# Gated block of a transformer stack: norms of later sequences placed beside the blocks of a square layer, and two more steps run ahead of a branch

## The chip, the cores and the metric

The kernel runs on one core of one Trainium2 chip. The metric is the device time of one launch in microseconds (us), the median of several runs. A core has a matrix engine (PE; its weight loads are listed as PEld), a vector engine (DVE), a scalar engine (ACT), GpSimd (POOL) and SyncE (SP), which here issues the DMAs. Each engine takes its instructions in the order in which the program emits them, and they wait for each other through semaphores.

## What is computed

Eight sequences of 512 positions by 128 features pass six layers of attention with a small MLP, and then a gated block. The change touches the gated block and the seam before it. Cut to what matters (`attn` is the six layers, `norm` subtracts the mean and divides by the root of variance plus 1e-5; `s1`, `s2`, ... are scales of each output feature):

```python
def reference(x, ...):                      # x: 8 x 512 x 128, f32
    x = x + attn(norm(x))
    v = norm(x)
    h = silu((v @ W1.T) * s1) * ((v @ W2.T) * s2)   # 128 -> 512
    h = gelu((h @ H1.T) * t1)                       # 512 -> 512
    h = gelu((h @ H2.T) * t2)                       # 512 -> 512
    return x + (h @ W3.T) * s3                      # 512 -> 128
```

The matrices W1, W2, H1 and H2 hold only -1, 0 and 1 in this input. The kernel looks at their low 12 bits at run time and takes the first of two arms of a branch (`gated_split`) if all are zero; that arm is the one that runs here.

## The kernel before, in words

**Attention.** The six layers of eight sequences are 48 units of 32 steps each. A step makes two score tiles on PE, takes their row maxima on DVE and their exponentials on ACT. All other work of a unit (projections, mixing, norms, MLP) is cut into small functions that are filed in the dictionary `later` under a step number and a place (`at`, L646); when the loop comes to a step, it emits what is filed there (`pending`, L652). A unit's work reaches some 76 steps past its own scores, so when the scores of the last unit end at step 1535, work is still filed from step 1536 on: the last mixing of the last unit, and the norms and MLPs of the last three units. `plan_group` (L735) and `plan_after` (L716) file it. Step 1536 holds one `gather` (L473) of the last unit and the `aggregate` of a norm; step 1537 holds `weights` (L462) of the last group of scores and `mix_values` and `mix_end` (L498, L506) of the last but one block of rows.

**Seam.** `finish(upto)` (L818) emits everything filed up to a step, in order. It is called with 1535, then the register with the low bits is read and the branch follows. What is left in `later` is emitted inside the arm, one step at a time, by `next_step` (L825).

**Gated block.** One `Gate` (L514) per sequence b has four stages. Stage 0 (`gate_stage`, L567) has four blocks; a block is four matmuls (named `q`), a silu on ACT (`sils`), a product on DVE (`gt`, L578) and a split. The split (L543) cuts a tile into a high and a low part: DVE masks the high part (`cut`, L549), POOL copies it into place (L550), and DVE subtracts it (L551); the parts are named `vs`, `fgs`, `h1s` by their tile. Stage 1 (`hidden_stage`, L584, the first square layer) has four blocks of eight matmuls (`qh`, L562), a gelu on ACT (`ht`, L598) and a split into `h1s`. Stage 2 (second square layer) has four blocks of eight matmuls and a gelu into `g`, with no split. Stage 3 (`end`, L603) has 32 matmuls (`fo`, L608), a product on DVE (`y`, L615), an addition on POOL (L619) and the DMA to `out`. After each block `run_stage` calls `next_step`, so that leftover steps lie between blocks. PSUM tiles of the matmuls come from a ring of six (`ring`, L179); transposes, MLP products and some others share one more (`one`, L176).

**The norm of a sequence** (`Gate.norm`, L530) is five calls in a row: `add` (L522; POOL adds the attention result to a fresh copy of x, the tile `x_out`, and makes the tile `v`), `stats` (four DVE statistics, L194), `aggregate` (four on DVE, L200, then two small POOL instructions, L201 and L202), `centre` (POOL, L205) and `scale` (POOL, L210). `turn` (L537) then transposes `v` on PE (`pt_w`, L217) and ACT copies it to `vT` (L541); `split_input` (L553) splits it into `vs` for stage 0. Gates 0 and 1 have had their norm in the attention loop; gates 2 to 7 get theirs in `gated_split` (L877).

**Order in `gated_split`.** Iteration b emits stage 0 of b, the whole norm of b+1, stage 2 of b-1, the turn and the split of b+1, stage 1 of b, stage 3 of b-1, and the load of `x_out` for b+2. `done(b)` (L831) names a step by which the attention result of b is complete; `finish(done(b+1))` stands ahead of the norm.

Of the kernel before, what the change touches and what calls it, by code (L numbers as in the profile page):

```python
# [9 lines left out]
F32 = mybir.dt.float32  # L10
# [7 lines left out]
P = 128  # L18
# [11 lines left out]
def attn_stack_then_ffn(ctx: ExitStack, tc: tile.TileContext, a: dict, out: bass.AP):  # L30
# [3 lines left out]
    B, L, E = x.shape  # L34
# [4 lines left out]
    LC = L // P  # L39
# [11 lines left out]
    work = ctx.enter_context(tc.tile_pool(name="work", bufs=2))  # L51
# [43 lines left out]
    def load_x(b, n):  # L95
        t = state.tile([P, LC, E], F32, tag="x", name=f"x_{n}", bufs=3)
        nc.sync.dma_start(t, x[b].rearrange("(c p) e -> p c e", p=P))
        return t
# [77 lines left out]
    def one(shape, n):  # L176
        return ps_one.tile(shape, F32, tag="one", name=n)
# [49 lines left out]
    U = len(units)  # L227
    PAIRS = LC * STRIPS * 2
# [285 lines left out]
    class Gate:  # L514
# [7 lines left out]
        def add(self):  # L522
            b = self.b
            self.x = xs.pop(b)
            nc.gpsimd.tensor_tensor(self.x, self.x, hs[b][:, :, 0:E], ALU.add)
            tag, bufs = ("vf", 1) if b < 2 else ("z1", None)
            self.v = work.tile([P, LC, E], F32, tag=tag, name=f"v_{b}", bufs=bufs)
            self.ln = Norm(self.x, self.v, f"f{b}")

        def norm(self):  # L530
# [107 lines left out]
    gates = [Gate(b) for b in range(B)]  # L638
# [107 lines left out]
    def step_rest(s):  # L746
        pending(s, PE_)
        pending(s, DVE_)
        pending(s, ACT_)

    def step_ring(s):
        for fn in later.pop((s, RING_), ()):
            fn()()
# [10 lines left out]
    xs = {}  # L764

    def load_out(b):
        if b < 2:
            xs[b] = load_x(b, f"out{b}")
        elif b < B:
            tag = ("hik", "lok", "hiq")[b % 3]  # L770
            xs[b] = work.tile([P, LC, E], F32, tag=tag, name=f"x_out{b}", bufs=1)
            nc.sync.dma_start(xs[b], x[b].rearrange("(c p) e -> p c e", p=P))

    for k in range(2 + 2 * HC):
# [4 lines left out]
    for b in range(2):  # L779
        gate, t = gates[b], (U - 2 + b) * PAIRS  # L780
        at(t - 4, DVE_, lambda b=b: load_out(b))
        at(t + 9, DVE_, gate.add)
        at(t + 14, DVE_, lambda gate=gate: gate.ln.stats(0, 2))
        at(t + 15, DVE_, lambda gate=gate: gate.ln.stats(2, LC))
        at(t + 26, DVE_, lambda gate=gate: gate.ln.aggregate())
        at(t + 28, DVE_, lambda gate=gate: gate.ln.centre())
        at(t + 29, DVE_, lambda gate=gate: gate.ln.scale())
# [30 lines left out]
    def finish(upto):  # L818

        for s in sorted({s for s, _ in later}):  # L820
            if s <= upto:
                step_rest(s)
                step_ring(s)

    def next_step():  # L825
        if later:
            s = min(s for s, _ in later)
            step_rest(s)
            step_ring(s)

    def done(b):  # L831

        return (U - B + b + 4) * PAIRS + 12

    def gated(b):
# [14 lines left out]
        for wt, sc, nm in ((fh1, "f_h1s_col", "h1"), (fh2, "f_h2s_col", "h2")):  # L850
            pool, tag = (proj, "qs") if nm == "h1" else (epool, "e")
            g2 = pool.tile([P, HC, L], F32, tag=tag, name=f"{nm}_{b}")
            for o in range(HC):
                ph = ring([P, L], f"p{nm}_{b}_{o}")
                for c in range(HC):
                    nc.tensor.matmul(
                        ph, wt[:, c, o * P : (o + 1) * P], gg[:, c, :],
                        start=(c == 0), stop=(c == HC - 1),
                    )
                nc.scalar.activation(g2[:, o, :], ph, AF.Gelu, scale=cols[sc][:, o : o + 1])  # L860
                if o == HC - 1 and 1 < b + 1 < B:
                    if nm == "h1":
                        load_out(b + 1)
                        finish(done(b + 1))
                        gates[b + 1].norm()
                    else:
                        gates[b + 1].turn(one([P, L], f"pt_v{b + 1}"))()
                next_step()
            gg = g2
        gates[b].end(gg)  # L870

    def run_stage(b, k):
        if 0 <= b < B:
            for _ in gates[b].stage(k):
                next_step()

    def gated_split():  # L877

        load_out(2)
        gates[0].split_input()  # L880
        next_step()
        for b in range(B + 1):
            run_stage(b, 0)
            if 1 < b + 1 < B:
                finish(done(b + 1))
                gates[b + 1].norm()
            run_stage(b - 1, 2)
            if b + 1 < B:
                if b + 1 > 1:
                    gates[b + 1].turn(one([P, L], f"pt_w{b + 1}"))()  # L890
                gates[b + 1].split_input()
            run_stage(b, 1)
            run_stage(b - 1, 3)
            if b + 2 > 2:
                load_out(b + 2)

    finish(U * PAIRS - 1)
    wide = nc.values_load(
        low_any, min_val=0, max_val=1 << 12,
        skip_runtime_bounds_check_because="it only chooses between two arms",  # L900
# [4 lines left out]
    with tc.If(wide < 1) as narrow:  # L905
        gated_split()
# [65 lines left out]
```

## Time and profile before

| | |
|---|---|
| median of 3 runs | 2724.29 us (2723.52 to 2725.32) |
| the profiled execution: its time | 2724.5 us |
| the profiled execution: its span, first to last instruction | 2722.4 us |
| mean granted PE clock, share of full speed | 0.992 |
| PE, DVE, ACT, POOL busy, share of the span | 97%, 91%, 92%, 69% |
| first matmul of stage 0 of sequence 0 | 2470.63 us after the start of the span |
| starts of stage 0 of sequences 4, 5, 6, 7 | 2590.38, 2620.57, 2651.01, 2681.76 us |

The span is the time between the first and the last instruction of one profiled execution; 2.1 us of the launch lie outside it. A share of busy time is a mean over two very different parts: about 2470 us of attention, in which the change alters nothing, and about 252 us of leftover steps and gated block, to which it belongs. The second part has to be read by its own rows, with a window that holds it alone. In a row of waits the engine named first stood idle until the instruction named after the arrow was done; columns are the total in us, the number of times and the longest.

### The profile page before, as it was taken

Reading aid. Unit: us, or ns where it says so; the run is one execution under the profiler, and the core shown is the slowest. Engines: PE = TensorE matmul, PEld = TensorE weight load, DVE = VectorE, ACT = ScalarE, POOL = GpSimd, SP = SyncE. Lnnn points to the kernel's source line nnn. Section 1 sums busy time; section 2 is a strip of 40 time slices with the busy share of each in tenths; the row PEclk is TensorE's granted clock in tenths of the full one; section 3 lists DMA queues with packets and bytes.
Section 4 is the critical chain, followed back from the end, with each engine's and each line's share of the span. In section 5 each row is a group of like instructions: output and inputs, shape, how many; then the busy total and the mean of one; then the engine's idle time right before and its main releaser. Section 6 shows DMA issues by size and latency. Waiting matters only on the chain.

```text
span 2722.4 us, 52066 instructions
## 1 busy us (share of the span) xinstructions
PE 2635.7 (97%) x14944; PEld 1377.4 (51%) x14944; DVE 2490.1 (91%) x6109; ACT 2495.2 (92%) x6846; POOL 1882.6 (69%) x2278
## 2 busy tenths in 40 slices
PE   6999999999999999999999999999999999998988
PEld 2445445445545545445445445445445445445776
DVE  6999999999999999999999999999999999997653
ACT  6999999999999999999999999999999999996343
POOL 5677777676676676676676676776776676676754
PEclk9999999999999999999999999999999999999989
DMA  6545444445444445444445444445445545440000
GB/s 147 116 104 133 96 107 109 100 103 125 101 102 109 99 104 126 104 98 109 102 101 126 105 98 108 107 98 124 106 100 119 124 118 132 110 93 5 16 16 21
DMA packets 135859, 273.78 MB, mean 101 GB/s; under 512 B 39696, under 2 KB 57232, under 8 KB 135568
## 3 DMA queue, kind: packets, MB, share of 16 engines
q1 hardware_dynamic: 133504, 269.31, 42.6%
q8 instruction: 122, 2.00, 0.3%
q10 hardware_dynamic: 2064, 1.08, 0.2%
q14 instruction: 169, 1.38, 0.2%
HBM read 13.86 MB, written 2.10 MB: 6 GB/s over the span
## 4 chain that ended last, share of the span: by engine, by line
PE 44%; ACT 32%; DVE 16%; issue 5%; POOL 2%; DMA 0%; ACTq 0%; SPq 0%; POOLq 0%; DVEq 0%
ACT e L455 27%; PE ps L441 13%; PE acc L476 12%; DVE top L450 11%; PE py L404 6%; PE po L501 3%; PE qh L562 3%; ACT g L394 2%; ACT w L483 2%; PE pk L260 2%; PE fo L608 1%; PE pt_w L217 1%; PE pq L269 1%; PE pt_h L217 1%; PE pt_u L217 1%
## 5 line engine op out<-in xcount | busy, mean ns | idle before, releaser
L455 ACT ACTIVATE e<-ps,top 128x512 f32<-128x512 f32 x3072 | 2125.0, 823 | 31.4 <-DVE top L450 15.0
L450 DVE TENSOR_REDUCE top<-ps 128x1 f32<-128x512 f32 x3072 | 1947.9, 680 | 35.6 <-PE ps L441 29.2
L441 PE MATMUL ps<-ks,qs 128*128 128x512 f32 x3040 | 1225.9, 477 | 25.6 <-ACT e L455 17.8
L455 ACT ACTIVATION_READ_ACCUMULATOR e<-ps,top 128x1 f32 x3072 | 1050.2, 342 | 0.0
L441 PEld LDWEIGHTS ps<-ks,qs 128*128 128x128 f32 x3040 | 489.3, 189 | 869.3 <-ACT e L455 652.6
L476 PE MATMUL acc<-e,rp 128*32 128x512 f32 x6144 | 819.1, 605 | 0.8 <-POOL rp L466 0.3
L466 POOL TENSOR_TENSOR rp<-pick,r 128x128 f32<-128x128 f32 x768 | 308.9, 402 | 532.5 <-DVE r L464 206.0
L476 PEld LDWEIGHTS acc<-e,rp 128*32 128x32 f32 x6144 | 121.2, 108 | 261.1 <-issue 134.1
L315 POOL TENSOR_TENSOR m<-loq,mask 128x512 f32<-128x512 f32 x190 | 243.2, 1280 | 0.0
L315 POOL TENSOR_TENSOR m<-hiq,mask 128x512 f32<-128x512 f32 x190 | 242.8, 1278 | 0.0
L501 PEld LDWEIGHTS po<-h,wT 128*128 128x128 f32 x1536 | 201.2, 192 | 20.1 <-DVE wT L493 3.9
L501 PE MATMUL po<-h,wT 128*128 128x129 f32 x1536 | 204.1, 276 | 1.0 <-DVE wT L493 1.0
L392 PE MATMUL pf<-uT,w 128*128 128x512 f32 x384 | 196.3, 592 | 0.3
L404 PEld LDWEIGHTS py<-w,g 128*128 128x128 f32 x1536 | 186.0, 192 | 10.8 <-DVE z L411 1.9
L404 PE MATMUL py<-w,g 128*128 128x128 f32 x1536 | 187.2, 275 | 1.0 <-DVE z L411 1.0
L394 ACT ACTIVATE g<-pf,b_col 128x512 f32<-128x512 f32 x192 | 164.8, 859 | 3.3 <-PE pf L392 3.3
L483 ACT ACTIVATE w<-acc 128x512 f32<-128x512 f32 x192 | 131.8, 686 | 22.3 <-PE acc L476 22.3
L464 DVE RECIPROCAL r<-zs 128x4 f32<-128x4 f32 x768 | 129.2, 168 | 4.4 <-ACT e L455 0.7
L493 DVE TENSOR_TENSOR wT<-pt_w,decay 128x512 f32<-128x512 f32 x192 | 126.9, 661 | 0.2
L279 POOL TENSOR_TENSOR loq<-qT,hiq 128x512 f32<-128x512 f32 x48 | 61.6, 1283 | 87.8 <-ACT e L455 67.1
L217 PE MATMUL pt_w<-ident,w 128*128 128x128 f32 x768 | 120.2, 279 | 0.6
L217 PEld LDWEIGHTS pt_w<-ident,w 128*128 128x128 f32 x768 | 88.2, 140 | 43.5 <-ACT g L394 30.1
(115 smaller groups left out, 2522.9 us busy)
## 6 DMA issues: line engine op xcount, KB each, us to landing
qs<-m SPq DMA_DIRECT2D x1520, 128.0 KB, 2.4
ks<-hik SPq DMA_DIRECT2D x384, 64.0 KB, 2.0
ks<-lok SPq DMA_DIRECT2D x376, 64.0 KB, 2.0
rows<-in_rows SPq DMA_DIRECT2D x6, 448.0 KB, 4.9
x_in<-in_x SPq DMA_DIRECT2D x8, 256.0 KB, 3.2
fh<-square SPq DMA_DIRECT2D x8, 256.0 KB, 2.3
x_out<-in_x SPq DMA_DIRECT2D x8, 256.0 KB, 3.0
out<-y SPq DMA_DIRECT2D x7, 256.0 KB, 2.4
```

What stands on the lines that cost most here:

```text
L217: nc.tensor.transpose(pt[:, c * P : (c + 1) * P], src[:, c, :], ident)
L315: nc.gpsimd.tensor_tensor(m[:, lc - 2 * two], part.unsqueeze(2).to_broadcast([P, NB, PER_STRIP, QB]), mask.unsqueeze(1).to_broadcast([P, N ...
L392: nc.tensor.matmul(pf, w1[:, f * P : (f + 1) * P], self.uT, start=True, stop=True)
L394: return lambda: nc.scalar.activation(self.g[:, f, :], pf, AF.Relu, bias=cols["b1_col"][:, k : k + 1])
L404: nc.tensor.matmul(self.py[:, k, :], self.g[:, f, c * P : (c + 1) * P], w2[:, f, :], start=(f == 0), stop=(f == FC - 1),)
L441: nc.tensor.matmul(ps[s], qs[:, nb * P : (nb + 1) * P].bitcast(F32R), un.ks[:, i, :].bitcast(F32R), start=True, stop=True,)
L450: nc.vector.tensor_reduce(top[s], ps[s], AX.X, ALU.max, negate=True)
L455: nc.scalar.activation(self.e[:, nb, :], ps[s], AF.Exp, bias=top[s], accum_out=self.zs[:, nb : nb + 1],)
L466: nc.gpsimd.tensor_tensor(self.rp, pick.unsqueeze(1).to_broadcast([P, NB, QB]), r.unsqueeze(2).to_broadcast([P, NB, QB]), ALU.mult,)
L476: nc.tensor.matmul(acc[nb * QB : (nb + 1) * QB, :], self.rp[:, nb, :], self.e[:, nb, :], start=(self.turn == 0), stop=(self.turn == STRIPS ...
L483: nc.scalar.activation(self.w.rearrange("p c l -> p (c l)"), acc, AF.Exp, scale=1.0 / H)
L501: nc.tensor.matmul(self.po, self.wT[:, c, :], self.unit.h[:, c, 0 : E + 1], start=(c == 0), stop=(c == LC - 1),)
```

## The change

In four parts:

1. **The norm is spread.** The norm of b+1 between stage 0 of b and stage 2 of b-1 goes. In its place the norm of b+2 is handed to stage 1 of b as a list of four functions (`norm_beside`): `add` after the first block, `stats` after the second, `aggregate` and `centre` after the third, `scale` after the fourth. Each is emitted ahead of that block's leftover step.
2. **Buffers.** `v` of every gate lies in the single buffer `vf` (before: gates 2 to 7 in the two buffers `z1`). `x_out` of gates 2 to 7 goes round four tags (before: three), of which `z1` is the fourth.
3. **Loads.** `x_out` of gates 2 and 3 is loaded at the start of the arm, and at the end of iteration b, from b = 1 on, that of b+3 (before: of gate 2 at the start, and of b+2).
4. **Seam.** Steps 1536 and 1537 are emitted ahead of the branch, and the one `next_step` between `split_input` of gate 0 and its stage 0 goes. Every later leftover step thereby comes one block earlier.

```diff
@@ Gate.add
-            tag, bufs = ("vf", 1) if b < 2 else ("z1", None)
-            self.v = work.tile([P, LC, E], F32, tag=tag, name=f"v_{b}", bufs=bufs)
+            self.v = work.tile([P, LC, E], F32, tag="vf", name=f"v_{b}", bufs=1)
@@ load_out
-            tag = ("hik", "lok", "hiq")[b % 3]
-            xs[b] = work.tile([P, LC, E], F32, tag=tag, name=f"x_out{b}", bufs=1)
+            tag = ("hik", "lok", "hiq", "z1")[b % 4]
+            bufs = None if tag == "z1" else 1
+            xs[b] = work.tile([P, LC, E], F32, tag=tag, name=f"x_out{b}", bufs=bufs)
@@
-    def run_stage(b, k):
+    def run_stage(b, k, beside=()):
+        beside = iter(beside)
         if 0 <= b < B:
             for _ in gates[b].stage(k):
+                next(beside, lambda: None)()
                 next_step()
+        for fn in beside:
+            fn()
+
+    def norm_beside(b):
+        if not 2 <= b < B:
+            return ()
+        finish(done(b))
+        gate = gates[b]
+        return (
+            gate.add,
+            lambda: gate.ln.stats(0, LC),
+            lambda: (gate.ln.aggregate(), gate.ln.centre()),
+            lambda: gate.ln.scale(),
+        )
@@ gated_split
         load_out(2)
+        load_out(3)
         gates[0].split_input()
-        next_step()
         for b in range(B + 1):
             run_stage(b, 0)
-            if 1 < b + 1 < B:
-                finish(done(b + 1))
-                gates[b + 1].norm()
             run_stage(b - 1, 2)
             if b + 1 < B:
                 if b + 1 > 1:
                     gates[b + 1].turn(one([P, L], f"pt_w{b + 1}"))()
                 gates[b + 1].split_input()
-            run_stage(b, 1)
+            run_stage(b, 1, norm_beside(b + 2))
             run_stage(b - 1, 3)
-            if b + 2 > 2:
-                load_out(b + 2)
-
-    finish(U * PAIRS - 1)
+            if b > 0:
+                load_out(b + 3)
+
+    finish(U * PAIRS + 1)
```

## Prediction

> **What bounds the kernel now.** I read the page first (the busy shares hide the gated block in a mean over the attention), then the waits of the gated part alone, then the chain of work that ended last through one iteration, then iterations and the granted clock in windows. Waits from 2480 us to the end, PE's two largest rows:
>
> ```profile
> PEld pt_w L217 <- POOL v L210: 28.9, 6, 7.3
> PE pt_w L217 <- POOL v L210: 25.9, 6, 6.5
> ```
>
> Six times, once for each of gates 2 to 7, the transposes of `v` stand at the head of PE until POOL has scaled `v`. PE's part is 25.9 us; the weight loads' row is the same stall. The chain through iterations 5 and 7 (start us, length us, what):
>
> ```profile
> 2629.82 1.14 POOL fgs L550
> 2630.96 1.26 POOL x_out L525
> 2632.24 0.87 DVE st_f L194 x4
> 2633.75 1.02 POOL rs_f L202
> 2634.77 1.02 POOL v L205
> 2635.86 1.05 POOL v L210
> 2636.95 1.11 PE pt_w L217 x4
> 2638.07 9.61 PE qh L562 x32
> 2647.68 3.57 PE fo L608 x32
> ...
> 2682.01 3.75 PE q L562 x16
> 2685.76 14.99 PE qh L562 x64
> ```
>
> The norm starts only after the last split of stage 0 (POOL is in order) and is one serial chain of 6 us over two engines. Iteration 7 has no norm: stage 0 is 3.75 us, two square layers are 14.99, so 7.5 each, with no idle time. In iteration 5 the square layer after the transposes took 9.61 us, 2.1 more for the same 32 matmuls. Windows (PE busy, PEld, DVE, ACT, POOL, then the clock) give the reason, and the length of whole iterations:
>
> ```profile
> 2606.00:2608.00 2.00, 1.25 (x5) 1.25 (x6) 0.00 (x0) 0.10 (x1) 0.70 (x1) 0.50 0.00 0
> 2608.00:2610.00 2.00, 2.00 (x6) 1.52 (x6) 1.12 (x2) 0.49 (x1) 0.98 (x1) 0.50 0.00 0
> 2612.00:2614.00 2.00, 2.00 (x10) 1.63 (x9) 1.12 (x2) 0.43 (x2) 1.14 (x1) 1.00 0.00 0
> ```
>
> ```profile
> 2651.00:2681.80 30.80, 25.56 (x120) 21.00 (x118) 14.93 (x31) 11.43 (x15) 15.97 (x15) 0.89 0.07 18
> 2681.80:2704.00 22.20, 22.20 (x113) 18.53 (x113) 12.65 (x21) 9.56 (x13) 10.32 (x9) 1.00 0.05 13
> ```
>
> After the wait PE runs at clock 0.50 for about 4 us. So a wait costs its length and then a slow start. An iteration with a norm takes 30.8 us, the one without 22.2, and POOL is busy for 16 us of the 30.8: it has room.
>
> **What the Trainium skill says.** "TensorE: Matmul & The Clock Gate", What's actually happening: an idle window of about 3.4 us halves PE's clock, and about 3.4 us of work restores it. The trace agrees: after waits of 4.9 to 6.5 us the next square layer takes 8.7 to 9.6 us, after one of 1.98 us the transposes take 0.66 instead of 1.11. "SBUF — State Buffer", Who interferes with whom: DVE operations in a 2-port mode or with two SBUF inputs, and GpSimd operations, exclude each other for a whole instruction. The trace agrees: a subtraction of 0.69 us takes 1.67 beside a POOL addition and ends only after it.
>
> ```profile
> 2528.79 1.48 POOL L376 TENSOR_TENSOR z<-z,b2s 128x512 f32<-128x512 f32 x1
> 2529.14 1.67 DVE L551 TENSOR_TENSOR fgs<-gt,cut_g 128x512 fp32r<-128x512 f32 x1
> ```
>
> **What part 1 removes.** The six waits (PE rows of the timeline) are 6.50, 1.98, 2.41, 4.89, 4.90 and 5.24, sum 25.9. Slow transposes, against 0.66: 0.45 + 0 + 0.10 + 3 x 0.45 = 1.9. Slow first square layers (8.68, none, 8.93, 9.37, 9.61, 9.60 against 7.5): 1.2 + 0 + 1.4 + 1.9 + 2.1 + 2.1 = 8.7. **At most 36.5 us** can be had here. With them gone an iteration is 3.75 + 7.5 + 0.66 + 7.5 + 3.57 = 23.0 us of PE work.
>
> What is late next? Stage 1 needs the last `fgs` cast, which ended 10.4 us after the start of stage 0 (2630.96 against 2620.57). PE would reach stage 1 after 3.75 + 7.5 + 0.66 = 11.9, and the fourth part is only its seventh matmul, 1.4 us on. So this isn't late, with 2.9 us to spare; iteration 7 shows it at work (cast end 2692.2, stage 1 at 2692.9).
>
> **What it adds beside stage 1.** Nothing new is executed: POOL's `add` 1.28, 0.20, 1.02, `centre` 1.04, `scale` 1.04, and DVE's 0.87 and 0.36 move behind the `h1s` splits. Queued behind them on POOL are the next block's cast and later `y`; on DVE the next `cut_h`; for `h1s` waits ACT's next gelu (its row of waits names L551). A stage 1 block has a chain of 2.06 us (2697.30 to 2699.37). Between an `h1s` and the next `cut_h` DVE has 0.91 us free: `stats` and the aggregation fit. POOL has 0.93 us free per block and gets 1.28, 0, 2.26 and 1.04. By the lock, block 1's cut waits for `add` (step to the next block about 2.8 us), and block 3's subtraction waits for `centre` (about 3.45). The last `h1s` comes 2.8 + 2.1 + 3.45 = 8.35 us after the first, before 3 x 2.06 = 6.2: 2.2 us late. Its first readers in order are DVE's `y` and `gt` of stage 0, which stand behind it: `gt` slips by some 0.9 us. The eighth `q` tile of the PSUM ring waits for the first `gt`, with 1.05 us to spare (2622.79 against 2623.84). So it is about hidden; I allow **0.3 us each in iterations 3, 4 and 5: 0.9**; uncovered, the full 2.2 each. The finished `v` is wanted some 14 us later: covered.
>
> **Iterations 0 to 2, where leftover steps share POOL.** Iteration 0: blocks get `add` + a scale, an affine, `aggregate` + `centre` + an affine, `scale` + a small norm step: 14 us of POOL with the casts, in a stage of 9.2 us of PE (two MLP products at 0.86). By the same stepping (cut at one POOL boundary, subtraction at the next) the blocks are 3.75, 2.75 and 3.45 apart, 10 us, against 7.7 in the trace (2486.75 to 2494.44), the first one 0.9 later. Then ACT's gelu, one relu more ahead of the silu (0.7), and `gt` give stage 2 of gate 0 at about 2500.0 instead of 2496.8: **a loss of 3.2**; between 1 and 5. Iteration 1 has the largest POOL load too. Its late `y` holds the first MLP addition, which stands behind it on DVE, and the second MLP product, which shares one PSUM tile with the first, waits for that: **2.0 lost**, of which 0.7 comes back since the same wait of before (1.0, PE at L404) shrinks. Net 1.3; between 0 and 4.
>
> **Parts 2 to 4.** `vf` alone: `centre` of b+2 must follow the transposes of b+1, which PE has done before that stage 1: 0. If not covered, a POOL wait of at most one stage. `x_out`: loads land 3.1 us after issue, behind the `out` DMA on SP, some 8 us ahead of `add`: 0; `z1` was free by then. Seam: ahead of the branch DVE's `mix_end` waits for `mix_values`, and the mask of `vs` is queued behind it, so stage 0 of gate 0 starts about 2.1 us later (2472.75 against 2470.63). But `mix_values` (0.9) no longer lies in it, and before PE stood 2.29 us at 2480 for the fourth `fgs`. That wait moves to the last mixing: ACT's exponential and its two table loads (1.28 each) come where they came before, and the first block of stage 1 is done within 0.6 us of before. The 0.9 us is part of the 3.2. The branch itself shows no gap (PE 0.16 us); behind a waiting DVE it may show 0 to 1.
>
> **Sum.** 36.5 - 3.2 - 1.3 - 0.9 = 31.1 us. The profiled execution was 2724.5 (span 2722.4 plus 2.1), 0.2 above the median; from the median, 2724.3 - 31.1 = **2693.2**.
>
> **Rivals.**
> A, the cover is short (0.20): lock and in-order queues stretch every stage 1 of iterations 0 to 5. For it: POOL's overload of iterations 0 and 1. Against it: two idle POOL stretches in each later iteration. If a block takes 3.5 us in all, the last `h1s` is 4.3 late, `gt` 3.4 and PE 2.4 in three iterations, and 1 to 2 more in each of the first: 10 to 12 us less gain, 2704; its band is 2699 to 2712.
> B, everything is covered (0.13): 2724.3 - 36.5 = 2687.8, or 2686 if stalls of before in iterations 0 to 2 go too.
> C, the wait only changes its name (0.03): POOL's lag carries into stage 0, and the last `fgs` cast lands 16.2 instead of 10.4 us after its start. Then stage 1 starts as late as now: 2724. It needs 5.8 us of lag where I find 1 to 1.5.
> D, slower (0.04): the load of `x_out` comes late. `add` waits on POOL, `stats` on DVE behind it, and with it the cuts of blocks 2 and 3: PE stops at stage 0 and again at stage 2, cold. It has some 8 us to spare; each us beyond costs one in each norm. It turns to slower when the loads land 8 + 31/6 = 13 us later than expected, that is 16 us after issue; at 18 us it gives 2724.3 - 31 + 6 x 7 = 2735. For it: SP issues it behind an `out` DMA that waits for `y`. Against it: 3.1 us measured.
>
> **Numbers.** My forecast (0.60) has its own range of 2688 to 2699: the ends of its three costs. The range for 8 in 10 takes in B and most of A's band: 2685 to 2706. Below 0.2% (5.4 us) a measurement of this kernel can hardly tell a change from none. Faster: forecast, A and B, 0.93; same: C, 0.03; slower: D, 0.04.
>
> **What would show it.** The row of PE waiting for L210 is gone; the clock stays at 1.00 in iterations 3 to 6; stage 0 starts are 23 us apart; the first square layer takes 7.5 us. Losses: stage 2 of gate 0 starts near 2500, not 2497; PE waits at L404 in iteration 2. Wrong if PE waits in the stage 0 matmuls for `gt` or a gelu by over 1 us in iterations 4 and 5 (A), in stage 1 for `fgs` (C), or DVE's statistics for a DMA (D).

## The result, and the profile after

The changed kernel takes **2688.35 us** (median of 4 runs, 2687.73 to 2689.64) against 2724.53 us (4 runs): 36.2 us less, a ratio of 0.9868 with a 95% interval of 0.9851 to 0.9885. Run again in a later set it took 2690.20 against 2724.19, which is 34.0 us less, a ratio of 0.9878 (0.9863 to 0.9893). The profiled execution took 2687.83 us with a span of 2686.0. The forecast was 2693.2 with a range of 2685 to 2706. So the direction and the main mechanism were right, and the gain was 3 to 5 us larger than the sum. The time is that of case B, "everything is covered". But not everything was covered: small losses remain, and small gains that the sum had left out make up for them, as the part after the experiments works out.

PE's waits in the gated part follow (engine, line and what it waited for: us in all, times, longest). Lines 528 to 769 of the kernel before have numbers one lower here, so that L561 is its L562:

```profile
PE po L501 <- DVE wT L493: 3.1, 1, 3.1
PE q L561 <- POOL vs L549: 2.7, 1, 2.7
PE qh L561 <- POOL h1s L549: 0.9, 1, 0.9
PE pt_w L217 <- ACT g L394: 0.9, 1, 0.9
```

The row of 25.9 us, `pt_w` behind POOL's `v`, is gone. What is left is small. The first two rows lie in iteration 0 and the third in iteration 1. In the last row, in iteration 2, the turn of gate 3 waits for an MLP tile that shares its PSUM place. The chain through one later iteration (start, length, what):

```profile
2581.52 7.49 PE qh L561 x32
2589.01 0.44 PE pt_w L217 x4
2589.44 7.49 PE qh L561 x32
2596.93 3.57 PE fo L607 x32
2600.50 3.75 PE q L561 x16
```

It never leaves PE: square layer, turn, square layer, output, stage 0. The square layer after the turn takes 7.49 us, as long as the other; before it took 9.4 to 9.6. The windows say the same with the clock (third figure from the end), for iterations 5, 6 and 7:

```profile
2600.30:2623.00 22.70, 22.70 (x118) 19.00 (x118) 16.54 (x31) 11.21 (x15) 15.99 (x15) 1.00 0.09 24
2623.00:2645.70 22.70, 22.70 (x118) 19.00 (x117) 14.61 (x23) 11.21 (x15) 13.88 (x14) 1.00 0.04 12
2645.70:2668.10 22.40, 22.40 (x116) 18.73 (x114) 12.39 (x21) 9.57 (x13) 10.33 (x9) 1.00 0.04 12
```

Iteration 5 has a norm beside its stage 1, iteration 6 has transposes but no norm, and iteration 7 has neither. Iterations 5 and 6 both take 22.7 us, so the norm costs PE nothing there; what iteration 7 saves are the transposes. The two traces side by side, by the start of a stage (matmul rows of the timeline); the last transposes ahead of the seam start at 2467.97 and 2468.19, so 0.2 us of every difference is drift of the attention:

| start of | before | after | earlier by |
|---|---|---|---|
| stage 0 of gate 0 | 2470.63 | 2473.53 | -2.9 |
| stage 2 of gate 0 | 2496.80 | 2498.17 | -1.4 |
| `fo` of gate 0 | 2522.32 | 2516.49 | 5.8 |
| `fo` of gate 1 | 2554.71 | 2547.72 | 7.0 |
| stage 0 of gate 4 | 2590.38 | 2577.52 | 12.9 |
| stage 0 of gate 5 | 2620.57 | 2600.26 | 20.3 |
| stage 0 of gate 6 | 2651.01 | 2623.00 | 28.0 |
| stage 0 of gate 7 | 2681.76 | 2645.74 | 36.0 |
| end of the span | 2722.4 | 2686.0 | 36.4 |

The seam loses 2.9 us at once, 2.7 without the drift, where 2.1 were reckoned. Iterations 4 to 6 bring 7.4, 7.7 and 8.0 us: their wait, their slow transposes and their slow square layer. This is the norm beside stage 1 in iteration 4 (timeline, in order of time):

```profile
2593.80 1.28 POOL L525 TENSOR_TENSOR x_out<-x_out,h 128x512 f32<-128x512 f32 x1
2594.01 1.35 DVE L548 TENSOR_SCALAR cut_h<-ht 128x512 int32<-128x512 int32 x1 [0.66 <-ACT ht L597]
2596.01 0.86 DVE L194 BATCH_NORM_STATS2 st_f<-x_out 128x6 f32<-128x128 f32 x4
2597.84 0.38 DVE L200 BATCH_NORM_AGGREGATE mv_f<-st_f 128x2 f32<-128x6 f32 x4
2598.13 0.55 DVE L548 TENSOR_SCALAR cut_h<-ht 128x512 int32<-128x512 int32 x1
2598.71 0.69 DVE L550 TENSOR_TENSOR h1s<-ht,cut_h 128x512 fp32r<-128x512 f32 x1
2598.81 1.47 POOL L202 TENSOR_TENSOR rs_f<-rs_f,neg_half 128x4 f32<-128x4 f32 x1
2600.26 1.04 POOL L205 TENSOR_TENSOR v<-x_out,mv_f 128x512 f32<-128x512 f32 x1
2601.25 0.60 POOL L549 CAST h1s<-cut_h 128x512 fp32r<-128x512 f32 x1
2601.82 1.04 POOL L210 TENSOR_TENSOR v<-v,rs_f 128x512 f32<-128x512 f32 x1
```

The second block's cut takes 1.35 us beside `add` and ends only after it, where the first block's, with no POOL operation beside it, took 0.43: this is the lock that the prediction reckoned with. But the fourth block's cut and subtraction (2598.13 and 2598.71) slip in right behind the aggregation, before POOL's long operations. Then it is POOL's power on 128x4 that is stretched, to 1.47 us from 1.02. The fourth block's copy on POOL, the other half of its `h1s`, has to stand in POOL's queue until 2601.25.

### The profile page after: what moved, and what is told of

The parts are those of the page before. It is cut to its first block, busy times and chain, and to the rows that moved or that the text cites. A ratio compares the mean times of both kernels' runs of the same rounds, so it can differ in the third digit from the quotient of the medians.

```text
span 2686.0 us, 52073 instructions
## 1 busy us (share of the span) xinstructions
PE 2622.3 (98%) x14944; PEld 1368.1 (51%) x14944; DVE 2501.6 (93%) x6109; ACT 2495.0 (93%) x6846; POOL 1883.4 (70%) x2278
## 4 chain that ended last, share of the span: by engine, by line
PE 47%; ACT 31%; DVE 16%; issue 5%; POOL 1%; DMA 0%; ACTq 0%; SPq 0%; POOLq 0%; DVEq 0%
ACT e L455 27%; PE ps L441 14%; PE acc L476 12%; DVE top L450 12%; PE py L404 6%; PE qh L561 4%; PE po L501 3%; ACT g L394 2%; ACT w L483 2%; PE pk L260 2%; PE fo L607 1%; PE q L561 1%; PE pq L269 1%; PE pt_w L217 1%; PE pt_h L217 1%
## 5 line engine op out<-in xcount | busy, mean ns | idle before, releaser
L450 DVE TENSOR_REDUCE top<-ps 128x1 f32<-128x512 f32 x3072 | 1947.8, 680 | 35.8 <-PE ps L441 29.2
L404 PEld LDWEIGHTS py<-w,g 128*128 128x128 f32 x1536 | 186.1, 192 | 8.6
L404 PE MATMUL py<-w,g 128*128 128x128 f32 x1536 | 186.9, 275 | 0.0
L483 ACT ACTIVATE w<-acc 128x512 f32<-128x512 f32 x192 | 131.8, 686 | 22.3 <-PE acc L476 22.3
```

The source lines that it names most:

```text
L404: nc.tensor.matmul(self.py[:, k, :], self.g[:, f, c * P : (c + 1) * P], w2[:, f, :], start=(f == 0), stop=(f == FC - 1),)
L450: nc.vector.tensor_reduce(top[s], ps[s], AX.X, ALU.max, negate=True)
L483: nc.scalar.activation(self.w.rearrange("p c l -> p (c l)"), acc, AF.Exp, scale=1.0 / H)
```

## The experiments

Each set of runs has its own runs of the kernel before (medians 2724.05, 2721.69 or 2724.19), and each gain below is taken against those of its set. Only the second run of experiment 8 and experiments 9 and 10 share a set with the changed kernel; between sets, gains are compared.

Two profiles of the changed kernel differ by 2.8 us from the last transposes to the end (217.8 and 220.6 us). In the second, PE's clock fell to 0.50 twice at the start of the arm, after the waits of 2.6 us for `vs` and of 3.1 us for `wT`; in the first it stayed at 1.00 after the same two waits. Here are the stretches after the two waits, first in the first profile, then in the second:

```profile
2476.19:2478.19 2.00, 2.00 (x13) 0.72 (x12) 1.61 (x4) 1.69 (x2) 1.14 (x1) 1.00 0.01 4
2484.19:2486.19 2.00, 2.00 (x14) 1.55 (x12) 1.82 (x6) 0.00 (x0) 1.21 (x2) 1.00 0.00 0
```

```profile
2475.12:2477.12 2.00, 2.00 (x8) 1.16 (x4) 0.73 (x2) 0.57 (x1) 1.14 (x1) 0.50 0.00 0
2485.12:2487.12 2.00, 2.00 (x7) 1.71 (x7) 1.91 (x4) 0.00 (x0) 2.00 (x2) 0.50 0.00 0
```

So a difference of under 3 us in iteration 0 is read only between profiles in which the clock did the same there.

The first theory was that part 1 alone makes the gain. The rival came out of the trace after: in the kernel before, ACT's gelu waited 17 times for the `h1s` of the block just before it, now only twice.

```profile
ACT ht L598 <- DVE h1s L551: 25.8, 17, 2.0
```

```profile
ACT ht L597 <- DVE h1s L550: 3.6, 2, 2.3
```

The likely reason is a buffer. In the kernel before, the mixing tile that step 1537 reads is alive at the branch. If its place, one of two `wT` buffers, then stays taken for the whole arm, all `gt` and `ht` tiles lie in the other. No trace shows buffers; experiments 1 to 3 test this by the wait that it would make.

**1. Without the seam** (parts 1 to 3 alone).

```diff
-    finish(U * PAIRS + 1)
+    finish(U * PAIRS - 1)
...
         gates[0].split_input()
+        next_step()
```

> The change without its seam (steps 1536 and 1537 come inside the arm again, with the one extra step after the first split). Found since the prediction: in the kernel before, the last mixing tile wT of step 1537 is alive at the branch, and one of the two wT buffers stays taken for the whole arm, so all gt and ht tiles share one. Theory 'part 1 alone' (the six waits and the cold clock are everything, the seam only costs its late start): 2686 to 2688, 0 to 2 us faster than the changed kernel. Rival 'the buffer carries the cover' (with one wT buffer ACT's gelu waits for h1s of the block before, and the norm's operations stretch that chain as in rival A): 2691 to 2697, with PE waits in stage 0 of iterations 3 to 5.

Measured: 2689.82 us (2688.44 to 2692.14) against 2724.05, ratio 0.9878 (0.9861 to 0.9894), a gain of 34.2. The gelu's wait is back, but PE does not wait behind it in the later iterations (ACT's row, then PE's largest):

```profile
ACT ht L597 <- DVE h1s L550: 31.8, 17, 3.7
...
PE py L404 <- DVE z L411: 2.4, 2, 2.0
```

Iterations 4 to 6 take 22.7 us here too (starts of stage 0 at 2579.04, 2601.77, 2624.51, 2647.25), so the rival named the wrong place. The time decides nothing: it lies between the two forecasts, 1.8 us above the one and 1.2 below the other. Parts 1 to 3 make 34.2 us where the whole change made 36.2 and 34.0, so these runs can't tell what the seam adds from nothing. PE's 2.0 us at L404 come in iteration 1; the account of the prediction returns to them.

**2. The seam alone**, with the norm in one piece.

```diff
-    finish(U * PAIRS - 1)
+    finish(U * PAIRS + 1)
...
         gates[0].split_input()
-        next_step()
```

> The kernel before with the seam alone (steps 1536 and 1537 ahead of the branch, no step after the first split); the norm stays in one piece. Theory 'part 1 alone': a loss of 0 to 2 us by the late start of stage 0 of gate 0, 2724 to 2726. Rival 'the buffer carries': both wT buffers go round, a block of stage 0 takes 1.92 instead of 2.14 us, so the last fgs cast and with it each norm come 0.7 to 0.9 us earlier in six iterations: a gain of 4 to 5 less the late start, 2720 to 2722.

Measured: 2727.66 us (20 runs) against 2724.05, ratio 1.0014 (1.0007 to 1.0021): slower by 3.6 us, a greater loss than either theory had. The profile is of the fastest run (2724.59). ACT's gelu waits for `h1s` only twice here. PE's waits for `v` stay, 26.6 us in six:

```profile
PE pt_w L217 <- POOL v L210: 26.6, 6, 6.8
PE po L501 <- DVE wT L493: 3.1, 1, 3.1
PE q L562 <- POOL vs L550: 2.6, 1, 2.6
```

The starts of stage 0 of gates 4 to 7 are 28.7, 29.6 and 28.6 us apart instead of 30.2, 30.4 and 30.8, so the second buffer does bring the norms forward, by 4.6 us in these three iterations; but the arm is 7.2 us late by then. Of this, 2.6 us are there when stage 2 of gate 0 starts. The other 4.6 come after that, up to stage 0 of gate 4, where the wait ahead of gate 4's turn is 4.8 us instead of 2.4. Why it grows was not tested. So the seam alone is a loss, and the rival's gain is real and smaller than that loss.

**3. The changed kernel with one buffer kept taken.**

```diff
+    pin = work.tile([P, L], F32, tag="wT", name="pin")
+    nc.vector.memset(pin[:, 0:1], 0.0)
...
     with tc.If(wide < 1) as narrow:
+        touch()          # copies pin[:, 0:1] into a small tile; also in the other arm
         gated_split()
```

> The changed kernel whole, and a tile in one of the two wT buffers that is written ahead of the branch and read once at the start of the arm, so that one buffer stays taken as in the kernel before. Nothing else moves. Theory 'part 1 alone': 2688 to 2689, as the changed kernel. Rival 'the buffer carries': 2691 to 2698, ACT waits for h1s again (some 17 to 20 times) and PE waits for gt or a gelu in stage 0.

Measured: 2692.98 us (2692.41 to 2695.22), ratio 0.9891 (0.9875 to 0.9908): a gain of 31.1, which is 2.9 to 5.1 us less than the changed kernel's two. The gelu's wait is back, so a tile that is alive at the branch is enough to bring it about:

```profile
ACT ht L597 <- DVE h1s L550: 29.3, 16, 2.9
```

The intervals of this and of the changed kernel overlap. The profiles say the same as the medians: this one and the first of the changed kernel both kept the clock at 1.00 at the start of the arm, and from the last transposes to the end they take 222.0 and 217.8 us. Of these 4.2 us, 2.4 are there at `fo` of gate 0, 3.6 at `fo` of gate 1 and no more at `fo` of gate 2. PE's waits there are new:

```profile
PE q L561 <- ACT sils L575: 1.8, 1, 1.8
PE qh L561 <- POOL fgs L549: 1.2, 1, 1.2
```

Later starts of stage 0 are 22.7 us apart again. In iteration 4 DVE's first and last `h1s` lie 6.8 us apart (2596.63 to 2603.42), with both buffers 6.05.

**4. The whole norm after the first block of stage 1.**

```diff
         return (
-            gate.add,
-            lambda: gate.ln.stats(0, LC),
-            lambda: (gate.ln.aggregate(), gate.ln.centre()),
-            lambda: gate.ln.scale(),
+            gate.norm,
         )
```

> The changed kernel, but the whole norm of b+2 stands after the first block of stage 1 and isn't spread. Theory 'spreading matters': DVE's four statistics and the second block's cut wait for add and POOL's chain, the last h1s comes about 3.5 us later, gt of stage 0 some 2.8 us later against about 1.1 us to spare, so 1.5 to 2 us of PE wait in each of iterations 3 to 5 and as much in 0 to 2: 2696 to 2700. Rival 'only the place matters, any order beside stage 1 is covered': 2687.5 to 2690.

Measured: 2699.27 us (2697.62 to 2702.09), ratio 0.9915 (0.9899 to 0.9932), a gain of 24.8, as the theory of spreading has it. The waits are those it names: `gt` and `y` stand late on DVE, and PE's PSUM ring behind them.

```profile
PE qh L561 <- DVE gt L577: 3.1, 1, 3.1
...
PE q L561 <- DVE y L614: 2.5, 3, 1.8
PE py L404 <- DVE z L411: 2.2, 1, 2.2
```

Iterations 4 to 6 lose 2.1, 0.6 and 0.6 us, where 1.5 to 2 were expected of each; the rest comes earlier in the arm.

**5. The whole norm after the fourth block.**

```diff
-            gate.add,
...
+            lambda: None, lambda: None, lambda: None, gate.norm,
```

> The changed kernel, but the whole norm of b+2 stands after the fourth block of stage 1. Theory 'spreading matters': DVE's y and gt of the next stage 0 stand behind the statistics, which wait for add, so gt comes about 1 us later than in the changed kernel, 0 to 0.7 us of PE wait per iteration, and the fgs casts stand behind scale on POOL: 2688 to 2693. Rival 'any order is covered': 2687.5 to 2689.

Measured: 2692.00 us (2690.47 to 2693.40) in a set where the kernel before took 2721.69, ratio 0.9887 (0.987 to 0.9903), a gain of 29.7. This is in the band of the theory of spreading and above that of its rival. By its profile it is 4.6 us over the second profile of the changed kernel, whose clock fell at the same two places, and 4.5 are there at the end of iteration 3. In the medians, late in the stage (29.7) is better than early (24.8), and spread (36.2 and 34.0) is best. The interval of this run overlaps with those of both neighbours; the intervals of early and spread do not overlap.

**6 and 7. More work on POOL.** `centre` gives the same result however often it runs.

```diff
-            lambda: (gate.ln.aggregate(), gate.ln.centre()),
+            lambda: (gate.ln.aggregate(), [gate.ln.centre() for _ in range(5)]),
```

(and `range(9)`.)

> The changed kernel with centre executed five times instead of once in the third block (the result is the same): 4 x 1.04 = 4.2 us of POOL more in each of six norms. Theory 'POOL has cover': POOL is busy 16 of 22.7 us in iterations 3 to 5, the fourth h1s cast and y come 4.2 us later and the fgs casts catch up by some 0.8 per block: 0 to 1 us per norm, 2688 to 2694. Rival A, the lock (each POOL operation more holds up a cut or a subtraction of DVE, and the chain has about 1 us to spare): 2 to 3 us per norm, 2700 to 2706.

> As the last, with centre nine times: 8.3 us of POOL more per norm, so that POOL would be busy 24.3 us of an iteration whose PE work takes 22.7. Theory 'POOL has cover up to its room': the bound changes to POOL, at least 1.6 us per later norm and 4 to 6 in iterations 0 and 1, where leftover steps load POOL: 2702 to 2716. Rival 'POOL is off the path whatever it does': under 2695.

Measured: 2704.12 us (2701.51 to 2704.69), ratio 0.993 (0.9913 to 0.9947), a gain of 17.6; and 2733.70, ratio 1.0043 (1.0026 to 1.0059), which is slower than the kernel before and far beyond the 2702 to 2716 expected. The first falls into the numbers of rival A, but not by its mechanism. Here are PE's waits of the two, and then a place in the first: the norm beside stage 1 of iteration 4, and PE in stage 2 of gate 4, which follows in iteration 5.

```profile
PE qh L561 <- POOL h1s L549: 10.7, 5, 4.5
```

```profile
PE qh L561 <- POOL h1s L549: 34.5, 6, 9.6
```

```profile
2614.13 5.92 POOL L205 TENSOR_TENSOR v<-x_out,mv_f 128x512 f32<-128x512 f32 x5
...
2620.00 0.61 POOL L549 CAST h1s<-cut_h 128x512 fp32r<-128x512 f32 x1
...
2620.66 6.35 PE L561 MATMUL qh<-h1s,fh 128*128 128x512 f32 x26 [1.14 <-POOL h1s L549]
```

The fourth `h1s` cast stands behind the `centre` calls on POOL, and stage 2, 26 matmuls from its end here, needs it. The prediction named `y` and `gt` on DVE as the first to feel a late split and passed over this reader. Four more took 4.9 us (5.92 less 1.04) and PE waited 1.14, so the cover was 3.7 us thick here, and as thick in iteration 6. It is thinner nearer to the leftover steps: in iteration 4 PE waited 3.64 us, so that only 1.2 was covered. With eight more PE waited 5.6 us in iterations 5 and 6, and the clock was 0.50 behind it.

**8. Gate 0's split ahead of the two steps**, still ahead of the branch.

```diff
-    finish(U * PAIRS + 1)
+    finish(U * PAIRS - 1)
+    gates[0].split_input()
+    finish(U * PAIRS + 1)
...
         load_out(3)
-        gates[0].split_input()
```

> The changed kernel with the split of gate 0's input put ahead of steps 1536 and 1537, still ahead of the branch, so that DVE's mask no longer stands behind mix_end, which waits for PE. Theory 'the seam's late start is paid for': stage 0 of gate 0 starts 1.5 to 2.4 us earlier, but its chain ends in the last mixing's exponential and two table loads on ACT; 0.5 to 2 us faster, 2686.3 to 2688. Rival 'the last mixing sets the start, the late split is hidden behind it': within 0.3 us of the changed kernel.

Measured: 2683.67 us (2681.61 to 2684.07) in the set with 2721.69, ratio 0.9859 (0.9842 to 0.9875), a gain of 38.0. The wait for `vs` is gone and stage 0 of gate 0 starts 2.7 us after the last transposes instead of 5.3. To settle it, it ran again beside the changed kernel.

> The changed kernel itself, as the yardstick for the other two of this set on the same chip: 35 to 37 us below the kernel before.

> The version with gate 0's split ahead of the two steps, again, beside the changed kernel on the same chip. From the profiles (the part from the last transposes of gate 1's v to the end is 215.3 us against 217.8) 2 to 3 us faster than the changed kernel; if that was chance, 0.

Measured: the changed kernel 2690.20 (2689.51 to 2690.63), this 2687.08 (2684.88 to 2687.59), so 3.1 us less, and no run of one in the range of the other; against the kernel before 0.9867 (0.9852 to 0.9882), a gain of 37.1. That is more than the 0.5 to 2 us of the theory, which saw the chain on ACT hide part of the late start. It hid none: between the profiles in which the clock stayed at 1.00, stage 1 of gate 0 starts 2.7 us earlier, as much as stage 0. This is the fastest version here.

**9. Two steps later** on top of that.

```diff
             for _ in gates[b].stage(k):
                 next(beside, lambda: None)()
-                next_step()
+                if (b, k) != (0, 0) or (n := n + 1) in (1, 4):
+                    next_step()
```

(`n` starts at 0.)

> As the last, and stage 0 of gate 0 takes leftover steps only after its first and fourth block, so that the last mixing's exponential comes after all four silus: one ACT table load less (1.28 us) in the chain to the fourth fgs. Theory 'that chain bounds the start': 1 to 2 us faster than the last. Rival 'the two steps that come later load POOL in iterations 0 to 2, which are full': 0 to 3 us slower than the last.

Measured: 2689.80 us (2688.88 to 2690.56), 2.7 over the last, with no run of one in the range of the other: the rival. PE now waits 4.6 us for the first MLP addition, at the place where I had put a loss of 2.0 for the change itself:

```profile
PE py L404 <- DVE z L411: 4.6, 1, 4.6
```

**10. The wait kept, the clock kept warm**: the kernel before, with matmuls that nobody reads in the time in which PE waits.

```diff
                 if b + 1 > 1:
+                    warm = ring([P, L], f"warm_{b}")
+                    for _ in range({1: 20, 2: 6, 3: 8}.get(b, 18)):
+                        nc.tensor.matmul(
+                            warm, fw1[:, 0:P].bitcast(F32R),
+                            gates[b].vs[:, 0, :].bitcast(F32R), start=True, stop=True,
+                        )
                     gates[b + 1].turn(one([P, L], f"pt_w{b + 1}"))()
```

> The kernel before with matmuls that nobody reads put on PE ahead of each turn, 20, 6, 8, 18, 18 and 18 of them (0.234 us each, 4.7 to 1.4 us in all, about what PE waits there), into a PSUM tile of the ring. The waits for the norm stay as long as they were; only PE isn't idle in them. Theory 'the cold clock is a cost of its own': the slow transposes and first square layers go, 1.9 + 8.7 us, less what the added matmuls overrun: 2713 to 2718 against 2724, clock 1.00. Rival 'the square layer after the turn is slow for another reason (gelu chain, PSUM ring)': 2723 to 2727.

Measured: 2715.35 us (2713.76 to 2717.86) against 2724.19, ratio 0.9969 (0.9958 to 0.998), a gain of 8.8. One of the waits and what follows it:

```profile
2628.45 4.37 PE L892 MATMUL warm<-vs,fw 128*128 128x512 f32 x18
2633.53 0.66 PE L217 MATMUL pt_w<-ident,v 128*128 128x128 f32 x4 [0.70 <-POOL v L210]
2633.94 7.73 PE L562 MATMUL qh<-fgs,fh 128*128 128x512 f32 x32
```

The norm comes no sooner (from the start of stage 0 of gate 5 to the turn that follows, both kernels take 16.4 us), yet the square layer takes 7.7 us in place of 9.96 in the same view before. So the slow start is a cost of its own, 8.8 us where 10.6 were reckoned, and useless work takes it away.

## Why the prediction was right, and where its sizes were off

- **What part 1 removes, "at most 36.5 us".** The mechanism was right in both halves: in experiment 1 the waits for `v` are gone and 34.2 us with them, and experiment 10 shows the cold clock apart. The size was 1.3 us too small, since warm transposes hold the chain for 0.44 us and not for 0.66, six times.
- **The clock.** The prediction says that the trace agrees with an idle window of about 3.4 us. It names waits of 4.9 us and more, and one of 1.98 after which nothing was slow. It leaves out the wait of 2.41 us in its own list, after which the square layer took 8.93. PE's clock was 0.50 there too, and also after the 2.29 us at 2480. So waits clearly shorter than 3.4 us were enough, and the measurement decides. The sum was not hurt, as it took the measured length of each layer.
- **Iterations 3 to 5, 0.9 us.** The loss was 0. On DVE, the stepping gave 8.35 us from the first `h1s` to the last; it measured 6.05. The first step was right (2.8 forecast, 2.74 measured), the last was not: 3.45 forecast, 1.48 measured. DVE's cut and subtraction came ahead of POOL's power and `centre`, where they had been reckoned to wait for both; and the gelu came early, since it no longer waits for the `h1s` before it (0.7 us by experiment 3). POOL's half did come as late as the stepping had it: the last copy starts 8.6 us after the first (2592.69 to 2601.25). The working took both halves for one.
- **Iterations 1 and 2, net loss of 1.3.** There was none. From stage 2 of gate 0 to `fo` of gate 2 the change gained 14.2 us by the two timelines (1.4 late, then 12.85 early), where the waits, transposes and slow layers of these iterations sum to 14.0. The 2.0 us for the first MLP addition were not lost, and before's 1.0 us at L404 went. The mechanism exists: without the seam PE waits 1.96 us at that place (experiment 1), and with two steps later 4.6 (experiment 9). In the changed kernel the steps come one block earlier, and the addition stands on DVE ahead of the first `gt` (2522.76 and 2523.24); in experiment 1 it stands behind that block's split. So the seam, which the prediction counted only as a late start, took this loss away.
- **Iteration 0, loss of 3.2.** The loss was 1.4 us at the start of stage 2, 1.2 without the drift. POOL's load was put down as the cause, but in experiment 1 the norm stands beside the same stage and stage 2 starts no later than before (28.7 and 28.8 us after the last transposes). The loss comes with the seam's order, and experiment 8 gets it back. In the first block of stage 2 PE waits 0.9 us more for the fourth copy; that wait is already taken off in the 14.2 above.
- **The seam.** The working saw its late start and missed two other effects: the buffer that it sets free in the arm (experiments 2 and 3), and the MLP addition. All three together are too small for experiment 1 to tell from nothing.
- **The cover.** "About hidden" was right, but only one of two guards was seen. What comes late on DVE meets PE through `gt` and `y`, as experiment 4 shows; what comes late on POOL meets it through the fourth copy into `h1s`, with 3.7 us to spare in iterations 5 and 6 and 1.2 in iteration 4.
- **The rivals and the signs.** B's number was met, and that is in part luck. From the last transposes to the end the profiles differ by 36.6 us. Waits, slow layers and transposes make 37.8 and the wait at L404 1.0; the late stage 2 of gate 0 takes off 1.2, and the waits of 0.9 us in iterations 1 and 2 take off 1.8. That makes 35.8. So losses that B denies are paid by gains that its sum left out. A's numbers came only with 4.9 us more of POOL per norm. D's place was quiet: the loads landed 3.0 us after issue, and no wait on them is seen. The signs of the gain all came: the row is gone, the clock is 1.00, stage 0 starts are 22.7 us apart. Of the two signs of loss, PE's wait at L404 did not come, and stage 2 of gate 0 started at 2498.2.

What stays open is why the seam alone lengthens the wait ahead of gate 4's turn, and what decides in a given execution whether the clock falls after a wait of 2 to 3 us.

## What to carry to other kernels

A wait of PE behind a serial norm cost its length and, most times, a slow start after it. Look for both in the windows, and for an iteration that has no such wait, which tells the floor (22.3 us here, 22.7 reached). Small operations moved beside a busy stage were best put one by one into the gaps between its blocks. Ask of each queue that they enter for all readers behind them: here DVE's and POOL's halves of one split had different readers and different room. Before work is moved across a branch, look which tiles are alive there, since each may hold a buffer in the arm, and look which later steps move with it.

## What the runs showed of the hardware

- The clock's fall is not fixed by the length of the wait alone. In the kernel before it fell to 0.50 after waits of 2.29 and 2.41 us and stayed at 1.00 after one of 1.98. After waits of 2.6 and 3.1 us at the start of the arm it fell in one profile of the changed kernel and stayed at 1.00 in the other; the two differ by 2.8 us.
- Matmuls that nobody reads kept the clock at 1.00: the square layer behind them took 7.7 us in place of 9.96.
- When a DVE and a POOL operation met, the one that came second was stretched: a cut of 0.43 us took 1.35 beside an addition on POOL, and a 128x4 power of POOL took 1.47 us in place of 1.02 beside a subtraction of DVE.
